# A graph layer by sorted running sums: each engine's order written out as lists, and scores taken by quarters of columns

## The chip, the cores and the metric

The kernel runs on one core of one Trainium2 chip. The metric is the time on the device in microseconds (us); lower is better. Before the change it is 2181.99 us, the median of three runs (2181.45 to 2182.83).

## What is computed

For each of B = 32 batches, `x` is a matrix of C = 512 rows (nodes) and N = 1024 columns. Two layers follow each other, each with a residual and a layer norm over the columns:

```python
# layer 0: attention whose score is a sum of one term per row and one per column
q = wq @ x[b];  k = wk @ x[b]                      # N values each
scores[m, n] = leaky_relu(q[n] + k[m])             # slope 0.01
agg = x[b] @ softmax(scores, axis=n).T
x1 = layernorm(x[b] + relu(adj @ agg + bm[:, None]))
# layer 1: adjacency again, its elements squared
out = layernorm(x1 + (adj * adj).T @ x1 + bias)
```

The softmax of such a sum needs no N x N matrix. For a given m, exp(leaky(q[n] + k[m])) is a product of a factor of n and a factor of m on either side of the sign change. So the kernel sorts the columns by q, builds running sums over the sorted columns from both ends, and looks up for each m the two sums at the place where the sign changes.

## The kernel before

Tiles have 128 partitions. CT = 4 is the number of row blocks of `x`, NT = 8 the number of column blocks, and `x` stays in SBUF for about four batches (`xp`, 4 buffers).

Each batch passes these stages. The short names in brackets are those of the lists that the change introduces; the text uses them with batch and index, so that `t.7.0` is turn 0 of batch 7.

1. **Scores.** `load` [ld] brings x in four DMAs. `scores_parts` [pa, copy pc] multiplies each row block by `wqk`, which holds wq and wk in two of 32 columns; the four row blocks use the four 32-column tiles of TensorE (L167) and are copied out by ScalarE (L173). `scores_cols` [co, copy cc] turns the result with eight 128 x 128 transposes (L180) and adds the four parts on VectorE (L183). `scores_row` [ro, copy rc] spreads q over all partitions by eight more transposes (L191) and copies it with its maximum (L194).
2. **Ranks and counts.** `ranks` [rk, end re] counts on VectorE for each column how many q's come ahead of it (L206). `counts` [ct, ends ce and we] does so on ScalarE for the place of the sign change (L218), then takes the factors of m (Exp, L229).
3. **Product and scatter.** `product` [z, copy zc] computes adj times x for one column block (L241, four matmuls of 512 columns, PSUM to `zt` by ScalarE, L245). `scatter` [sc] writes the rows of `zt` to DRAM at their ranks, by an indirect DMA that GpSimd issues (L250).
4. **Sums.** `sums_load` [sl] reads the sorted rows back in two DMAs; `sums_exp` [se], `sums_up` [u] and `sums_down` [d] form the running sums of eight columns in each partition on VectorE (L284, L293). `carry` [cu and cd, copies uc and dc] adds up over partitions by matmuls (L310, copied out by L311); `table_up` [tu, te] and `table_down` [td] add the carries (L316), and the table goes to DRAM in two large DMAs and a small one [tw, tl].
5. **Lookup.** `gather` [g] fetches 128 table rows by an indirect DMA (L339), eight in a batch. `mix_weights` [mw] (L352 to L356) and `mix` [ms on ScalarE L361, mx on VectorE L362] combine the two sums.
6. **Layer 0 end.** `layer0` turns the mixed rows back [t, eight transposes each, L389], adds relu and residual on VectorE [r, L390] and takes the mean (L369); `layer0_spread` [s0] sums squares on ScalarE (L374), `layer0_root` and `layer0_end` [rt, rce] give the inverse deviation, by which the squared adjacency is scaled [w, L409].
7. **Layer 1.** `layer1` [l, row block m, half h; L418] multiplies, `layer1_out` adds the bias [b, L428], `layer1_spread` sums squares [s1] and takes the root on GpSimd [r1, L380, L381, L440], `layer1_scale` normalizes [n, L444], `layer1_store` writes [st].

Each engine runs its instructions in the order in which the program issues them; there is no scheduler (`manual_schedule`). One loop over i sets this order: iteration i has the product of batch i, the scores of i + 1, the lookup of i - 1 and the layers' end of i - 2, with a few steps of i - 3. The same code serves the first and last iterations, by conditions on i. SP issues all plain loads and stores in that order, GpSimd all indirect DMAs. [...]`p2` has three buffers of two banks (scores, turns, layer 1), `p1` two buffers of one bank (product, carries).

Of the kernel before, what the change touches and what calls it, by code (L numbers as in the profile page):

```python
# [25 lines left out]
F32 = mybir.dt.float32  # L26
# [14 lines left out]
def adj_resnorm_kernel(  # L41
# [15 lines left out]
    NH = N // H  # L57
# [8 lines left out]
    s3 = ctx.enter_context(tc.tile_pool(name="s3", bufs=3))  # L66
    dr = ctx.enter_context(tc.tile_pool(name="dr", bufs=1, space=bass.MemoryType.DRAM))
    p2 = ctx.enter_context(tc.tile_pool(name="p2", bufs=3, space=bass.MemoryType.PSUM))
    p1 = ctx.enter_context(tc.tile_pool(name="p1", bufs=2, space=bass.MemoryType.PSUM))
# [10 lines left out]
    load(0)  # L80

# [55 lines left out]
    def weights():  # L137
        nc.vector.tensor_scalar(nbm, nbm, -1.0, None, ALU.mult)
        for r, a in enumerate(adj_in):
            t = p1.tile([P, CT, P], F32, tag="m", name=f"adj_tp_{r}")  # L140
            for c in range(CT):
                nc.tensor.transpose(t[:, c, :], a[:, c * P : (c + 1) * P], ident)
            nc.vector.tensor_copy(adj_t[:, :, r * P : (r + 1) * P], t)
        for r, a in enumerate(adj_in):
            nc.vector.tensor_tensor(adj_2[:, r, :], a[:, 0:C], a[:, 0:C], ALU.mult)
            nc.vector.tensor_tensor(
                adj_2[:, r, r * P : (r + 1) * P], adj_2[:, r, r * P : (r + 1) * P], ident, ALU.add
            )
# [7 lines left out]
    class Batch:  # L156
        pass
# [4 lines left out]
    def scores_parts(b):  # L162
        s, xt = st[b], xts[b]
        t4 = p2.tile([P, N], F32, tag="w", name=f"qk_ps_{b}")
        for h in range(NH):
            for c in range(CT):
# [80 lines left out]
    def scatter(b, j):  # L247
# [7 lines left out]
        )  # L255


    def sums_load(b):


        s = st[b]
# [319 lines left out]
```

## Time and profile before

| | |
|---|---|
| median of 3 runs | 2181.99 us |
| profiled execution, its own time | 2177.85 us |
| its span, first to last instruction | 2176.1 us |
| mean granted TensorE clock | 0.981 |
| TensorE (PE) busy | 2078.4 us, 96% |
| VectorE (DVE) busy | 1678.2 us, 77% |
| ScalarE (ACT) busy | 1277.4 us, 59% |
| GpSimd (POOL) busy | 901.3 us, 41% |
| DMA | 541.53 MB, mean 249 GB/s |

The profile comes from one execution. Its slices divide the span into 40 equal parts and give the busy share in tenths, 9 meaning 90% or more. A group line gives source line, engine, operation, output and inputs, the count, the busy time with the mean of one instruction, and the idle time ahead with what ended it. In order of time, a line gives start, length, engine, source line and operation, and in brackets the idle time ahead with its releaser. PE's instructions overlap, so that the difference of two starts is a better price than the length of one.

### The profile page before, as it was taken

The page shows a single profiled execution, that of the slowest core. Times are in us where ns is not written, and L with a number is a line of the kernel's source. Part 1 is how long each engine was busy: PE and PEld are TensorE (multiplying, and loading weights), DVE is VectorE, ACT ScalarE, POOL GpSimd, SP SyncE. Part 2 cuts the span into 40 slices and gives each one's busy share as a digit, 9 for nine tenths or more (in the row PEclk, how much of TensorE's full clock was granted, in tenths as well). Part 3 has the DMA queues.
Part 4 walks back from the last instruction along what each step waited for, and adds up shares of the span by engine and source line. Part 5 has one row for each costly group of instructions (what it writes and reads, how often), then busy time and mean ns, then how long its engine had stood idle before and what let it go on. Part 6 is the DMA issues. An engine that isn't in the chain of part 4 may idle for free. (4 is left out here: it accounts for less than half of the span.)

```text
span 2176.1 us, 21481 instructions
## 1 busy us (share of the span) xinstructions
PE 2078.4 (96%) x6416; PEld 1008.9 (46%) x6416; DVE 1678.2 (77%) x2965; ACT 1277.4 (59%) x2142; POOL 901.3 (41%) x1037
## 2 busy tenths in 40 slices
PE   5759999999999999999999999999999999999976
PEld 2324444444444444444444444444444444444433
DVE  4677877878778878878787977787887788787562
ACT  2346666556666556666655666655666665566443
POOL 1223445444344434444543434443444453444431
PEclk9879999999999999999999999999999999999988
DMA  3566787666787667678777668776667866766751
GB/s 121 197 227 234 268 300 265 253 254 230 256 292 290 250 256 255 236 274 301 258 255 263 237 245 296 284 260 252 252 237 272 300 257 252 256 241 255 258 197 68
DMA packets 139705, 541.53 MB, mean 249 GB/s; under 512 B 16034, under 2 KB 16034, under 8 KB 131396
## 3 DMA queue, kind: packets, MB, share of 16 engines
q1 hardware_dynamic: 79936, 336.42, 40.8%
q0 software_dynamic: 57344, 202.15, 27.4%
q10 hardware_dynamic: 2308, 1.58, 0.2%
q8 instruction: 51, 0.84, 0.1%
q14 instruction: 66, 0.54, 0.1%
HBM read 270.80 MB, written 269.29 MB: 248 GB/s over the span
## 5 line engine op out<-in xcount | busy, mean ns | idle before, releaser
L241 PE MATMUL z_ps<-adj_t,x 128*128 128x512 f32 x2048 | 916.1, 598 | 5.2 <-ACT zt L245 4.3
L418 PE MATMUL l_ps<-x,w 128*128 128x512 f32 x2048 | 894.1, 595 | 16.8 <-DVE w L409 16.8
L418 PEld LDWEIGHTS l_ps<-x,w 128*128 128x128 f32 x2048 | 390.7, 191 | 496.6 <-issue 492.0
L241 PEld LDWEIGHTS z_ps<-adj_t,x 128*128 128x128 f32 x2048 | 380.8, 191 | 474.7 <-issue 451.3
L250 POOL DMA_INDIRECT sorted_z<-zt,to x256 | 275.6, 1076 | 408.5 <-ACT zt L245 235.9
L380 POOL TENSOR_SCALAR sd<-var 128x1 f32<-128x1 f32 x128 | 93.1, 728 | 702.4 <-ACT junk L374 701.1
L206 DVE SCALAR_TENSOR_TENSOR junk_v<-qk,qkc,tie 128x1024 uint8<-128x1024 f32 x256 | 328.3, 1283 | 7.0
L339 POOL DMA_INDIRECT got<-table,of x256 | 268.1, 1047 | 132.8 <-issue 69.9
L390 DVE SCALAR_TENSOR_TENSOR x<-agg_ps,nbm,x 128x1024 f32<-128x1024 f32 x128 | 163.9, 1280 | 179.8 <-PE agg_ps L389 179.8
L218 ACT ACTIVATE junk_s<-qk,qkc 128x1024 bf16<-128x1024 f32 x256 | 294.2, 1149 | 13.8 <-DVE qk L194 9.6
L444 ACT ACTIVATE g<-g,nb,rs 128x1024 f32<-128x1024 f32 x128 | 158.9, 1241 | 179.4 <-POOL spare L473 91.8
L245 ACT COPY zt<-z_ps 128x512 f32<-128x512 f32 x256 | 148.6, 581 | 179.2 <-PE z_ps L241 178.9
L361 ACT ACTIVATE got<-got,w 128x512 f32<-128x512 f32 x256 | 163.4, 709 | 112.4 <-DVE w L356 112.4
L381 POOL TENSOR_TENSOR rs<-sd,power 128x1 f32<-128x1 f32 x128 | 217.4, 1698 | 10.7
L374 ACT ACTIVATE junk<-x,nmean 128x1024 bf16<-128x1024 f32 x128 | 147.3, 1151 | 96.6 <-DVE nmean L369 95.7
L362 DVE SCALAR_TENSOR_TENSOR got<-got,w 128x512 f32<-128x512 f32 x256 | 175.1, 746 | 35.4 <-ACT got L361 35.4
L374 ACT ACTIVATE junk<-g,nmean 128x1024 bf16<-128x1024 f32 x128 | 146.3, 1143 | 92.9 <-DVE nmean L369 92.1
L428 DVE SCALAR_TENSOR_TENSOR g<-l_ps,bias_b 128x1024 f32<-128x1024 f32 x128 | 156.3, 1221 | 31.2 <-PE l_ps L418 30.3
L293 DVE SCALAR_TENSOR_TENSOR tab<-tab,ac 128x513 f32<-128x513 f32 x224 | 168.6, 753 | 8.0
L389 PEld LDWEIGHTS agg_ps<-ident,got 128*128 128x128 f32 x1024 | 121.1, 143 | 70.3 <-issue 62.2
L284 DVE SCALAR_TENSOR_TENSOR tab<-tab,ac 128x514 f32<-128x514 f32 x192 | 144.9, 755 | 9.7 <-ACT ac L273 1.3
L316 DVE TENSOR_TENSOR tab<-tab,carry 128x2052 f32<-128x2052 f32 x64 | 143.8, 2288 | 0.0
(76 smaller groups left out, 1315.5 us busy)
## 6 DMA issues: line engine op xcount, KB each, us to landing
table<-tab SPq DMA_DIRECT2D x64, 2056.0 KB
tab<-sorted_z SPq DMA_DIRECT2D x64, 1028.0 KB
x<-in_x_dram SPq DMA_DIRECT2D x128, 512.0 KB
out_dram<-g SPq DMA_DIRECT2D x128, 512.0 KB
sorted_z<-zt,to POOLq DMA_INDIRECT x256, 5.4
got<-table,of POOLq DMA_INDIRECT x256, 5.8
adj<-in_adj_dram ACTq DMA_DIRECT2D x4, 256.0 KB
bias_b<-in_L_gnn_bias_dram ACTq DMA_DIRECT2D x1, 512.0 KB
```

What stands on the lines that cost most here:

```text
L206: nc.vector.scalar_tensor_tensor(junk, s.qb, s.q[:, j : j + 1], tie[:, at : at + N], ALU.subtract, ALU.is_gt, accum_out=s.rank[:, j : j + 1],)
L218: nc.scalar.activation(junk, s.qb, AF.Sign, bias=s.k[:, j : j + 1], accum_out=s.sign[:, j : j + 1])
L241: nc.tensor.matmul(t, xt[:, c, j * P : (j + 1) * P], adj_t[:, c, :], start=(c == 0), stop=(c == CT - 1),)
L250: nc.gpsimd.indirect_dma_start(out=sorted_z[b % 2][:, :], out_offset=bass.IndirectOffsetOnAxis(ap=s.to[:, j : j + 1], axis=0), in_=zt[:, j ...
L293: nc.vector.scalar_tensor_tensor(zs[:, j, 0:D], zs[:, j, 0:D], s.ac[:, 1, j : j + 1], zs[:, j + 1, 0:D], ALU.mult, ALU.add,)
L339: nc.gpsimd.indirect_dma_start(out=s.got[:, j, :], out_offset=None, in_=table[b % 2][:, :], in_offset=bass.IndirectOffsetOnAxis(ap=s.of[:, ...
L361: nc.scalar.activation(down, down, AF.Copy, scale=w[:, 1, j : j + 1])
L362: nc.vector.scalar_tensor_tensor(up, up, w[:, 0, j : j + 1], down, ALU.mult, ALU.add)
L374: nc.scalar.activation(junk, t, AF.Square, bias=v[1][:, i : i + 1], accum_out=v[2][:, i : i + 1])
L381: nc.gpsimd.tensor_tensor(v[4][:, at], v[3][:, at], power[:, at], ALU.pow)
L390: nc.vector.scalar_tensor_tensor(t[:, o, :], ps, nbm[:, o : o + 1], t[:, o, :], ALU.max, ALU.add, accum_out=s.v0[0][:, o : o + 1],)
L418: nc.tensor.matmul(s.ps[m][:, at], s.w2[:, n, m * P : (m + 1) * P], t[:, n, at], start=(n == 0), stop=(n == CT - 1),)
```

## The change

The loop with its conditions is gone. Every step is a small function with a short name, and three lists of words give the order in which the steps are issued: `head` for the first batches, `loop`, which is repeated 17 times, and `tail` for the last. A word is a step's name, a batch relative to a base, and the step's indices; the base is 0 for the head, 10 to 26 for the loop and 32 for the tail, so that `t.-3.0` in the loop with base 10 is `t.7.0`, and `l.-2.0.0` in the tail is `l.30.0.0`. Steps that were one function are now two where they run on two engines (a product and its copy, a mix's scaling and its sum). The order of each engine, SP and GpSimd included, follows from the lists alone.

The scores change too. `parts` gives each of the four column tiles of TensorE a quarter of the columns instead of a row block, and sums over the row blocks in PSUM; two transposes are then enough, and VectorE copies instead of adding. The means are no longer computed apart: the Square takes the plain sum as its bias and -N as its scale, and the root divides by N cubed. `p1` now has four buffers and `p2` two. At the start, the three weight vectors come as rows and are turned on TensorE, the adjacency comes in one DMA on SP ahead of x, its squares are formed on GpSimd, half of the copies of the turned adjacency go to ScalarE, and the bias is loaded from inside the head list.

The diff, cut to its core:

```diff
-    p2 = ctx.enter_context(tc.tile_pool(name="p2", bufs=3, space=bass.MemoryType.PSUM))
-    p1 = ctx.enter_context(tc.tile_pool(name="p1", bufs=2, space=bass.MemoryType.PSUM))
+    p2 = ctx.enter_context(tc.tile_pool(name="p2", bufs=2, space=bass.MemoryType.PSUM))
+    p1 = ctx.enter_context(tc.tile_pool(name="p1", bufs=4, space=bass.MemoryType.PSUM))
...
+    adj_in = one.tile([P, NT, 2 * ZR], F32, tag="got", name="adj_in")[:, 0:CT, 0:C]
+    nc.sync.dma_start(out=adj_in, in_=adj.rearrange("(r p) c -> p r c", p=P))
+    load(0)
...
-    def scores_parts(b):
-        s, xt = st[b], xts[b]
-        t4 = p2.tile([P, N], F32, tag="w", name=f"qk_ps_{b}")
-        for h in range(NH):
-            for c in range(CT):
-                nc.tensor.matmul(
-                    t4[32 * c : 32 * c + 32, h * H : (h + 1) * H], wqk[:, c, :],
-                    xt[:, c, h * H : (h + 1) * H], start=True, stop=True,
                 )
...
+    def parts(b):
+
+        s = st[b]
+        s.ps = p1.tile([P, C], F32, tag="m", name=f"qk_ps_{b}")[:, 0:Q]
+        for c in range(CT):
+            for g in range(CT):
+                nc.tensor.matmul(
+                    s.ps[32 * g : 32 * g + 32, :], wqk[:, c, :],
+                    xts[b][:, c, g * Q : (g + 1) * Q], start=(c == 0), stop=(c == CT - 1),
                 )
...
+    def cols(b):
+        s = st[b]
+        s.ps = p1.tile([P, C], F32, tag="m", name=f"qk_tp_{b}")[:, 0:Q]
+        for k in range(Q // P):
+            at = slice(k * P, (k + 1) * P)
+            nc.tensor.transpose(s.ps[:, at], s.part[:, at], ident)
...
-    def mean(i, v):
-        nc.vector.tensor_scalar(v[1][:, i : i + 1], v[0][:, i : i + 1], -1.0 / N, None, ALU.mult)
...
         nc.scalar.activation(
-            junk, t, AF.Square, bias=v[1][:, i : i + 1], accum_out=v[2][:, i : i + 1]
+            junk, t, AF.Square, bias=v[0][:, i : i + 1], scale=-float(N),
+            accum_out=v[1][:, i : i + 1],
         )
...
-        nc.gpsimd.tensor_scalar(v[3][:, at], v[2][:, at], 1.0 / N, EPS, ALU.mult, ALU.add)
-        nc.gpsimd.tensor_tensor(v[4][:, at], v[3][:, at], power[:, at], ALU.pow)
...
+        nc.gpsimd.tensor_scalar(v[1][:, at], v[1][:, at], 1.0 / N**3, EPS, ALU.mult, ALU.add)
+        nc.gpsimd.tensor_tensor(v[1][:, at], v[1][:, at], power[:, at], ALU.pow)
...
-    for i in range(B + 3):
-        new, cur, old, past = i + 1 < B, i < B, 0 <= i - 1 < B, 0 <= i - 2 < B
...
+    def emit(words, base):
+        for word in words.split():
+            name, b, *at = word.split(".")
+            ops[name](base + int(b), *map(int, at))
+            if name in pool_ops:
+                pool_last[0] = "scatter" if name == "sc" else None
+
+    head = """
+    ld.1 ld.2 pa.0 z.0.1 pc.0 co.0 zc.0.1 pa.1 cc.0 z.0.6 ro.0 z.0.0 rc.0 rk.0.0 ct.0.3 ct.0.4
+    rk.0.3 z.0.2 ct.0.7 rk.0.2 pc.1 oq.0 ct.0.2 rk.0.5 z.0.3 zc.0.0 rk.0.1 zc.0.2 zc.0.6 rk.0.6
+    rk.0.7 z.0.4 zc.0.3 ct.0.6 rk.0.4 re.0 sc.0.0 co.1 zc.0.4 z.0.5 cc.1 ct.0.5 sc.0.6 ct.0.1
+    sc.0.2 sc.0.4 ro.1 zc.0.5 ct.0.0 sc.0.1 z.0.7 ce.0 sc.0.5 rc.1 we.0 sc.0.3 rk.1.3 z.1.3
+    zc.0.7 ct.1.4 sc.0.7 rk.1.4 rk.1.1 z.1.0 rk.1.2 sl.0.0 rk.1.5 sl.0.1 ld.3 oq.1 rk.1.7 z.1.6
+    rk.1.6 rk.1.0 se.0.0 z.1.1 ct.1.7 u.0.0 u.0.1 zc.1.3 u.0.2 se.0.1 zc.1.6 u.0.3 zc.1.0 pa.2
...
+    z.3.7 ms.0.5 d.1.3 zc.3.0 mx.0.3 ms.0.7 d.1.2 zc.3.3 zc.3.6 mx.0.5 mx.0.7 cu.1 d.1.1 z.3.2
+    uc.1 mx.0.6 zc.3.7 mx.0.4 tu.1.1 t.0.0 d.1.0 t.0.1 r.0.0 cd.1 r.0.1 t.0.3 dc.1 oq.3 s0.0.1
+    t.0.2 td.1.1 sc.3.3 z.3.1 s0.0.0 r.0.2 zc.3.2 tw.1.1 r.0.3 s0.0.2 z.3.5 tu.1.0 s0.0.3 rt.0
+    td.1.0 z.3.4 we.1 rce.0 tw.1.0 w.0.0 w.0.3 w.0.1 w.0.2 te.1 l.0.3.0 tl.1 l.0.1.0 sl.2.0
+    g.1.0 sl.2.1 g.1.1 l.0.3.1 g.1.3 g.1.2 g.1.6 l.0.1.1 b.0.3 g.1.5 s1.0.3 g.1.4 ct.3.5 l.0.0.0
+    b.0.1 g.1.7 se.2.0 zc.3.4 u.2.0 sc.3.0 zc.3.5 u.2.1 sc.3.7 se.2.1 u.2.2 ct.3.3 l.0.2.0
...
+    u.2.6 ms.1.3 mx.1.0 s1.0.1 u.2.7 l.0.2.1 ct.3.2 r1.0.1 mx.1.3 mw.1.1 b.0.0 ms.1.4 ms.1.7
+    r1.0.3 mx.1.2 ms.1.6 cu.2 ld.4 mx.1.4 ms.1.5 mx.1.7 s1.0.0 mx.1.5 mx.1.6 r1.0.0 b.0.2 t.1.1
+    d.2.7 s1.0.2 t.1.0 r.1.1 uc.2 r1.0.2 r.1.0 t.1.3 n.0.1 d.2.6 n.0.3 t.1.2 d.2.5 sc.3.1 s0.1.0
+    z.4.0 d.2.4 sc.3.2 n.0.0 d.2.3 s0.1.1 d.2.2 st.0.0 st.0.3 r.1.2 pa.4 n.0.2 d.2.1 st.0.2
+    z.4.2 ce.3 d.2.0 we.3 s0.1.2 r.1.3 pc.4 zc.4.0 te.2 tu.2.1 cd.2 tl.2 zc.4.2 st.0.1 co.4 dc.2
...
+    loop = """
+    g.-3.3 rk.-1.1 ct.-1.4 g.-3.4 rk.-1.0 g.-3.6 z.-1.3 rk.-1.5 g.-3.7 b.-4.0 g.-3.5 oq.-1
+    rk.-1.6 l.-4.2.0 se.-2.0 rk.-1.4 u.-2.0 u.-2.1 l.-4.3.0 mw.-3.0 rk.-1.3 ms.-3.1 zc.-1.3
+    se.-2.1 re.-1 u.-2.2 ms.-3.2 l.-4.2.1 ms.-3.0 mx.-3.1 zc.-1.2 mx.-3.0 ct.-1.1 mx.-3.2 u.-2.3
+    l.-4.3.1 b.-4.2 mw.-3.1 u.-2.4 ms.-3.4 ms.-3.7 u.-2.5 l.-4.1.0 ms.-3.3 mx.-3.4 ms.-3.6
+    u.-2.6 ms.-3.5 b.-4.3 ct.-1.6 mx.-3.6 s1.-4.0 l.-4.1.1 mx.-3.5 s1.-4.3 mx.-3.3 r1.-4.0
+    mx.-3.7 s1.-4.2 u.-2.7 t.-3.0 d.-2.7 ld.0 ct.-1.7 r1.-4.2 d.-2.6 cu.-2 ct.-1.5 b.-4.1 z.-1.0
+    d.-2.5 s1.-4.1 sc.-1.3 d.-2.4 r.-3.0 r1.-4.3 t.-3.2 zc.-1.0 d.-2.3 uc.-2 z.-1.1 n.-4.2
+    d.-2.2 sc.-1.0 d.-2.1 st.-4.2 r1.-4.1 d.-2.0 r.-3.2 t.-3.1 zc.-1.1 n.-4.0 cd.-2 tu.-2.1
+    sc.-1.1 st.-4.0 t.-3.3 dc.-2 n.-4.3 sc.-1.2 pa.0 r.-3.1 ct.-1.0 st.-4.3 td.-2.1 z.-1.6
+    ct.-1.3 s0.-3.0 te.-2 tw.-2.1 r.-3.3 z.-1.7 tu.-2.0 s0.-3.3 zc.-1.6 td.-2.0 s0.-3.1 sc.-1.6
+    z.-1.5 pc.0 s0.-3.2 tw.-2.0 tl.-2 rt.-3 co.0 zc.-1.7 z.-1.4 rce.-3 cc.0 zc.-1.5 w.-3.0
+    n.-4.1 w.-3.2 w.-3.1 ce.-1 st.-4.1 w.-3.3 l.-3.0.0 zc.-1.4 we.-2 sc.-1.4 sc.-1.5 ro.0
+    sc.-1.7 z.0.2 rc.0 g.-2.0 g.-2.2 ct.0.2 rk.0.7 g.-2.1 sl.-1.0 rk.0.2 l.-3.0.1 sl.-1.1
+    """
+    tail = """
...
+    zc.-1.3 mx.-3.5 l.-4.2.1 dc.-2 sc.-1.3 mx.-3.7 td.-2.1 z.-1.5 b.-4.2 tw.-2.1 td.-2.0 t.-3.0
+    zc.-1.5 tu.-2.0 s1.-4.2 t.-3.1 ct.-1.6 r.-3.0 z.-1.4 r1.-4.2 tw.-2.0 st.-4.0 r.-3.1 s0.-3.0
+    sc.-1.5 t.-3.2 zc.-1.4 s0.-3.1 sc.-1.4 t.-3.3 r.-3.2 n.-4.2 r.-3.3 l.-4.1.0 s0.-3.2 st.-4.2
+    te.-2 s0.-3.3 ce.-1 tl.-2 we.-1 sl.-1.0 rt.-3 sl.-1.1 l.-4.1.1 rce.-3 g.-2.0 g.-2.2 w.-3.0
+    g.-2.1 w.-3.2 se.-1.0 w.-3.3 w.-3.1 b.-4.1 g.-2.3 l.-3.3.0 g.-2.5 u.-1.0 s1.-4.1 u.-1.1
+    g.-2.4 u.-1.2 se.-1.1 l.-3.3.1 g.-2.6 u.-1.3 u.-1.4 g.-2.7 u.-1.5 u.-1.6 l.-3.2.0 u.-1.7
+    mw.-2.0 d.-1.7 ms.-2.2 b.-3.3 ms.-2.1 l.-3.2.1 ms.-2.3 d.-1.6 ms.-2.0 mx.-2.1 d.-1.5 mx.-2.0
+    l.-3.1.0 mx.-2.2 mw.-2.1 mx.-2.3 ms.-2.5 b.-3.2 ms.-2.6 ms.-2.7 mx.-2.6 l.-3.1.1 s1.-3.2
+    mx.-2.7 d.-1.4 ms.-2.4 s1.-3.3 mx.-2.5 d.-1.3 r1.-3.3 mx.-2.4 d.-1.2 t.-2.0 b.-3.1 r1.-3.2
+    d.-1.1 n.-3.3 t.-2.2 r.-2.0 cu.-1 d.-1.0 t.-2.1 s0.-2.0 r1.-4.1 r.-2.2 cd.-1 uc.-1 r.-2.1
+    t.-2.3 s0.-2.2 tu.-1.1 l.-3.0.0 s0.-2.1 dc.-1 n.-4.1 r.-2.3 s1.-3.1 st.-4.1 td.-1.1 l.-3.0.1
+    s0.-2.3 r1.-3.1 td.-1.0 tw.-1.1 rt.-2 n.-3.1 rce.-2 tu.-1.0 w.-2.0 tw.-1.0 w.-2.2 w.-2.3
+    w.-2.1 b.-3.0 l.-2.0.0 te.-1 s1.-3.0 tl.-1 n.-3.2 r1.-3.0 l.-2.2.0 st.-3.2 st.-3.3 g.-1.0
+    l.-2.0.1 g.-1.1 g.-1.2 g.-1.3 l.-2.2.1 b.-2.0 g.-1.4 g.-1.5 l.-2.3.0 b.-2.2 g.-1.6 mw.-1.0
+    g.-1.7 ms.-1.3 ms.-1.2 l.-2.1.0 ms.-1.0 n.-3.0 mx.-1.0 mx.-1.2 ms.-1.1 st.-3.0 s1.-2.0
+    st.-3.1 mx.-1.1 l.-2.3.1 mx.-1.3 s1.-2.2 r1.-2.0 mw.-1.1 ms.-1.7 ms.-1.6 mx.-1.7 ms.-1.4
+    l.-2.1.1 mx.-1.6 r1.-2.2 ms.-1.5 b.-2.3 mx.-1.5 mx.-1.4 n.-2.2 b.-2.1 t.-1.0 r.-1.0 t.-1.1
+    r.-1.1 t.-1.2 s0.-1.0 r.-1.2 t.-1.3 s0.-1.1 r.-1.3 s0.-1.2 s0.-1.3 rt.-1 s1.-2.3 rce.-1
+    w.-1.0 w.-1.2 s1.-2.1 w.-1.3 w.-1.1 n.-2.0 l.-1.1.0 r1.-2.1 st.-2.0 n.-2.1 l.-1.0.0 st.-2.1
+    st.-2.2 l.-1.1.1 l.-1.0.1 b.-1.1 s1.-1.1 r1.-1.1 l.-1.2.0 b.-1.0 s1.-1.0 r1.-2.3 l.-1.3.0
+    r1.-1.0 n.-2.3 l.-1.2.1 st.-2.3 n.-1.0 n.-1.1 l.-1.3.1 b.-1.2 st.-1.1 st.-1.0 s1.-1.2
+    r1.-1.2 b.-1.3 s1.-1.3 n.-1.2 r1.-1.3 st.-1.2 n.-1.3 st.-1.3
+    """
     weights()
...
+    emit(head, 0)
+    for b in range(10, B - 5):
+        emit(loop, b)
+    emit(tail, B)
```

## The prediction

> **What bounds the kernel now.** I read the page's slices first, then the time in stretches of 64 us, then TensorE in order of time.
>
> ```profile
> PE   5759999999999999999999999999999999999976
> DVE  4677877878778878878787977787887788787562
> ```
>
> TensorE is full from slice 5 to slice 38; VectorE nowhere is.
>
> ```profile
> 64.00:128.00 64.00, 38.83 (x111) 17.53 (x109) 38.32 (x61) 26.10 (x51) 21.67 (x24) 0.82 0.61 228
> 128.00:192.00 64.00, 49.68 (x162) 24.94 (x163) 47.17 (x80) 30.58 (x55) 16.90 (x19) 0.86 0.67 242
> 1024.00:1088.00 64.00, 63.97 (x201) 31.16 (x200) 51.83 (x93) 39.60 (x68) 28.90 (x32) 1.00 0.71 257
> 2048.00:2112.00 64.00, 48.33 (x130) 24.23 (x130) 43.00 (x75) 26.34 (x43) 20.61 (x21) 0.84 0.59 221
> 2112.00:2176.00 64.00, 45.63 (x123) 21.37 (x121) 20.33 (x45) 26.72 (x37) 7.60 (x24) 0.87 0.16 66
> ```
>
> The columns after the length are PE, PEld, DVE, ACT, POOL, then granted clock, DMA share and GB/s. In mid-run PE has 63.97 of 64 us. At both ends it has 39 to 50, at a lower clock too. So two things can shorten this kernel: less PE work in each batch, and fewer holes at the ends.
>
> ```profile
> 729.40 3.70 PE L241 MATMUL z_ps<-adj_t,x 128*128 128x512 f32 x8
> 732.94 1.04 PE L389 MATMUL agg_ps<-ident,got 128*128 128x128 f32 x8
> 733.90 1.92 PE L167 MATMUL qk_ps<-x,wqk 128*32 128x512 f32 x16
> 735.76 3.70 PE L241 MATMUL z_ps<-adj_t,x 128*128 128x512 f32 x8
> 739.30 1.04 PE L389 MATMUL agg_ps<-ident,got 128*128 128x128 f32 x8
> 740.17 1.04 PE L180 MATMUL qk_tp<-ident,qk 128*128 128x128 f32 x8
> 741.04 3.60 PE L241 MATMUL z_ps<-adj_t,x 128*128 128x512 f32 x8
> ```
>
> From start to start this prices PE: z 3.43 us for a j, parts (L167) 1.86, eight transposes 0.87. A half of `layer1` is 3.43 and a carry 0.87 by the same view. The first z after a layer 1 begins at 724.03 in this batch and at 788.30 in the next: the period is **64.27 us**. The sum is 8 x 3.43 + 8 x 3.43 + 4 x 0.87 + 2 x 0.87 + 1.86 + 0.87 + 0.87 = 63.7, so 0.55 us a batch are small waits.
>
> ```profile
> 142.29 2.05 PE L310 MATMUL carry_ps<-end,before 128*128 128x257 f32 x4 [23.55 <-DVE end L284]
> ...
> 2093.57 29.98 PE L418 MATMUL l_ps<-x,w 128*128 128x512 f32 x64 [10.37 <-DVE w L409]
> 2123.39 3.97 PE L389 MATMUL agg_ps<-ident,got 128*128 128x128 f32 x32
> 2133.76 30.36 PE L418 MATMUL l_ps<-x,w 128*128 128x512 f32 x64 [6.40 <-DVE w L409]
> ```
>
> The holes: PE waits for chains on VectorE that have no other PE work over them. The steady order begins at 209.20 (batch 3's first z); the PE work done by then is worth 134 us (three batches of z 82, one layer 1 27.5, four scores 14.5, turns, carries, weights 10), so the **start costs 75 us**. After 2010.53 there remain 122 us of PE work (z 27.5, three layer 1 82.5, turns and carries 12), and PE ends at 2164: 31 us lost, and 12 more to the span's end. The **end costs 43 us**. Check: 32 x 63.7 + 2 + 75 + 43 + 28 x 0.55 = 2174, against a span of 2176.1.
>
> **What the Trainium skill says.** "TensorE: Matmul & The Clock Gate", Part 3 (packing small matmuls), says that matmuls in different column tiles run at once. The trace agrees: 16 passes of 0.592 us each take 1.86 us together. The same page, Part 1, says an idle window halves the PE clock; the clock of 0.82 to 0.87 beside the holes agrees. "Perfetto Trace Analysis", Optimizing Tensor Performance, says that independent groups should rotate through PSUM banks; the waits list has the next z's load waiting for a carry's copy (L311) 30 times, 13.0 us in all, with two `p1` buffers.
>
> **The change part by part.**
>
> *Scores by quarters.* Parts go from 8 matmuls of 512 columns to 16 of 256, c outside and the four column tiles inside. A 257-column pass takes 0.380 us against 0.592 (carry rows), and four carry passes 0.87. Packed four wide, 8 groups x 0.218 = 1.74; nearest row 1.86; unpacked 32 x 0.218 = 7.0. I take 1.86, no gain. The sum over c is now in PSUM, so `cols` is 2 transposes, not 8: 6 x 0.109 = **0.65 us a batch off PE**, 21 us in all. The copy out is 256 columns (0.375 by the L311 row) for two of 0.578, and DVE's reduce of 0.217 becomes a copy of like size; both lie beside PE work.
>
> *No separate means.* 256 instructions of L369 go, 39.4 us of DVE, 1.2 a batch. The Square takes the sum as its bias and -N as a constant scale; root and `nb` keep three POOL operations. Nothing on PE waits for a mean in mid-run, since DVE is busy 51.8 of 64. Worth: 0.15 on each chain at the ends. I count nothing, between -1 and +1 us.
>
> *PSUM.* `p1` has 4 buffers, `p2` 2. `p1` frees the waits for carry copies (0.4 of the 0.55). With two, `p2` needs `biased` or `residual` prompt: in the loop list `l.6.1.0` waits for `b.6.2` (1.30 us) while `l.6.3.1` runs 3.43 us. Cost 0 while that cover holds.
>
> *Loop order* (names with base 10, position 0 at its start, PE units added up). The list has z and layer 1 mixed. Three covers decide. (1) `t.7.3` ends at 36; then `r.7.3` behind `td.8.1`, four Squares among two counts, a table load with Sqrt (1.6) and four `w` (1.7) end near 50.2; `l.7.0.0` is due at 52. (2) `ld.10` follows `l.6.1.1` at 24 and `pa.10` is at 36: 12 us, where now 9.7 (724.22 to 733.90) suffice. (3) Eight gathers stand together on POOL behind `sc.9.7`, from about -6.5, beside the two sums loads. The last batch now shows such a burst alone: begun near 2095.5, `w` released at 2110.78, 15.2 us for 4.2 MB. With 2.1 MB of sums, 21 us at 300 GB/s, the rate of the busiest slices: they land at 14.5. `mw.7.1` and its mixes need about 9, `t.7.0` is due at 24. All three are covered, the first and third by one or two us. On SP, `ld.10` stands ahead of the stores and of both table writes, which are issued from 39 and 45: its wait ends at 24. On POOL the four `r1` (2.7 each) stand ahead of scatters whose last goes at 56. I take 0.7 us of waits a period, between 0.2 and 2.
>
> *Start.* The copies of the turned adjacency are shared by DVE and ACT (0.69 each), its squares move to POOL, whose first scatter comes near 43, and the bias is loaded on SP behind the first table write (0.5 MB; first read at 160): nothing for these, up to 2 us if POOL is slow. x0 landed at 15.9; now the 1 MB of adjacency is ahead of it on SP's queue instead of beside it on ACT's: PE begins near 17. `pa.1` waits 3 us for x1. Then z of batches 0 to 3 cover the first chain: PE has 115 us of listed work ahead of `t.0.0`, t = 134. On DVE, ranks and sums end near 67, the table is written near 100, gathers are in at 115, mixes end near 132. `l.0.3.0`, at 151, needs `w` by 148. One wait has no cover: `ld.4` is behind the whole of layer 1 of batch 0 and `z.4.0` comes 4.3 us later, where a load takes 9.7: 5 us. With 2 for clock, **27 instead of 75**.
>
> *End.* Now three layer 1 are left after the last z, with holes. In the list, at `z.31.4`, 103 us of PE work are left, in which the last batch's table and gathers lie. Two holes stay: `l.30.0.0` comes 6.9 us (two halves of `l.29.0`) after `t.30.3`, whose chain is about 12: 5 us; `l.31` behind `t.31`: 6.4 as now. With 2 for slow clock, 2 for `t.31` behind gathers, 12 after the last matmul: **27 instead of 43**.
>
> *Sum.* 32 x 63.05 = 2017.6, weights 2, start 27, end 27, 27 periods x 0.7 = 19: span 2092.6. The profiled run lies 1.75 over its span (2177.85 against 2176.1): 2094. The median of before is 4.1 over its profiled run, so about 2098; I forecast **2096**.
>
> **The rivals.**
>
> *The periods gain nothing.* Cover (1) or (3) fails by up to 2.5 us: a period of 64.3 to 66.3. For: one or two us is less than POOL's L381 varies (1.1 to 2.5 us in one batch). Against: DVE has 12 us free in each. 27 x 0.6 to 2.5 more: 2112 to 2165. The ends still gain.
>
> *The ends fill half.* The lists count on chains that start on time, and an engine in order behind one late load delays all. 75 + 43 then go to about 86 instead of 54: 2128.
>
> *Slower: the gather burst.* Gathers, sums loads and table writes meet, and `t.7.0` waits for mixes in every period. It decides from 3.1 us of added wait a period (84 us / 27). If the 6.3 MB move at 250 GB/s (25 us) and the table lands 3 us later, the burst ends at 21.7, the mixes at 30.7, and `t.7.0`, due at 24, stalls 6.7 us in each period, 6 more than I keep: 2096 + 27 x 6 = 2258. Against: the DMA share is 0.71 now at 257 GB/s.
>
> *The quarters don't pack.* Parts serial, 7.0: 32 x 5.1 = +163, 2259. Against: the column tiles are the same as now.
>
> **How the numbers follow.** Forecast 0.60 (2070 to 2114), no gain in periods 0.20, half-filled ends 0.11, burst 0.07, no packing 0.02. The range is 2070 to 2148: it keeps the forecast, the second and most of the first rival. 0.2% is 4.4 us, about what a measurement of this kernel can tell from no change. Only the last two cases and a little of the first are slower: faster 0.89, same 0.02, slower 0.09.
>
> **What would show it.** Right: L167's successor with 1024 passes of about 0.38 and about 1.9 us a batch; `qk_tp` with 64 transposes; a period near 63.7; PE at 9 from the second slice; a wait of about 5 us for x near 180; holes of some 5 and 6 us before the last two layer 1. Wrong: a period over 65, with PE waiting for `w` or `got`; parts of several us; a DMA share that rises while PE idles.

## The result, and the profile after

The changed kernel takes **2082.72 us**, the median of 4 runs (2081.17 to 2087.41), against 2181.72 us (2181.39 to 2182.83) for the kernel before, measured beside it: a ratio of 0.9549, with a 95% interval of 0.9532 to 0.9566. It is faster by 99 us. The profiled execution took 2081.17 us, its span is 2079.4 us and its mean granted clock 0.994.

The slices of the page of the changed kernel, to be held against those of before:

```profile
PE   8999999999999999999999999999999999999986
DVE  4879879777788777788777887777887778777762
PEclk9999999999999999999999999999999999999998
```

TensorE is now full from the second slice on; before it was so from the fourth. VectorE has the same share of a shorter span. Only the last two slices still dip. The time in stretches of the changed kernel (the columns after the length are PE, PEld, DVE, ACT, POOL, granted clock, DMA share, GB/s):

```profile
64.00:128.00 64.00, 64.00 (x211) 31.48 (x210) 56.84 (x95) 37.05 (x70) 31.71 (x38) 1.00 0.63 239
128.00:192.00 64.00, 62.64 (x217) 31.05 (x216) 49.62 (x77) 38.65 (x68) 23.07 (x33) 1.00 0.74 288
1024.00:1088.00 64.00, 64.00 (x213) 31.39 (x212) 49.85 (x85) 38.28 (x67) 28.00 (x33) 1.00 0.69 267
1952.00:2016.00 64.00, 57.68 (x156) 26.72 (x155) 43.77 (x73) 29.06 (x49) 26.99 (x31) 0.97 0.65 248
2016.00:2080.00 64.00, 46.72 (x124) 21.50 (x122) 20.88 (x41) 30.49 (x42) 8.28 (x24) 0.87 0.27 107
```

Where PE had 38.83 and 49.68 of 64 us in the second and third stretch before, it has 64.00 and 62.64, and at full clock. At the end the last stretch but one gains (57.68 against 48.33), and the last is much as it was (46.72 against 45.63). TensorE of the changed kernel in order of time, in mid-run:

```profile
1039.17 1.04 PE L432 MATMUL agg_ps<-ident,got 128*128 128x128 f32 x8
...
1051.37 1.93 PE L171 MATMUL qk_ps<-x,wqk 128*32 128x256 f32 x32
1053.23 10.57 PE L260 MATMUL z_ps<-adj_t,x 128*128 128x512 f32 x24
1063.64 0.38 PE L186 MATMUL qk_tp<-ident,part 128*128 128x128 f32 x2
1063.85 3.60 PE L260 MATMUL z_ps<-adj_t,x 128*128 128x512 f32 x8
...
1102.50 1.04 PE L432 MATMUL agg_ps<-ident,got 128*128 128x128 f32 x8
```

From `t.x.0` to `t.x.0` is 1102.50 - 1039.17 = **63.33 us**. Before, the period was 788.30 - 724.03 = 64.27 us, from the first product after a layer 1 to the next:

```profile
724.03 3.60 PE L241 MATMUL z_ps<-adj_t,x 128*128 128x512 f32 x8
...
788.30 3.60 PE L241 MATMUL z_ps<-adj_t,x 128*128 128x512 f32 x8
```

The score parts take 1053.23 - 1051.37 = 1.86 us, as before, and the transposes of the columns 0.21 instead of 0.87. The same view, where PE still waits (the bracket gives the idle time ahead of the line and what ended it):

```profile
171.08 1.09 PE L432 MATMUL agg_ps<-ident,got 128*128 128x128 f32 x8 [0.63 <-DVE g L480]
...
1908.57 5.40 PE L260 MATMUL z_ps<-adj_t,x 128*128 128x512 f32 x8 [3.37 <-ACT zt L266]
...
1998.26 29.43 PE L469 MATMUL l_ps<-x,w 128*128 128x512 f32 x64 [2.83 <-DVE w L460]
...
2036.75 30.68 PE L469 MATMUL l_ps<-x,w 128*128 128x512 f32 x64 [3.94 <-DVE w L460]
```

The two holes at the start in which carries waited 39.2 us together, 23.55 of it in the one shown before, are gone; after the 7.01 us that TensorE waits for its first load, the largest is now 3.94 us. The two `layer1` at the end take 29.43 and 30.68 us for work that takes 27.5 in mid-run: there the clock is below full.

### The profile page after: what moved, and what is told of

Same layout as the page of the kernel before. It is cut to its first block, busy times and chain, and to the rows that moved or that the text cites. A ratio compares the mean times of both kernels' runs of the same rounds, so it can differ in the third digit from the quotient of the medians.

```text
span 2079.4 us, 21612 instructions
## 1 busy us (share of the span) xinstructions
PE 2042.6 (98%) x6737; PEld 1000.6 (48%) x6737; DVE 1609.8 (77%) x2700; ACT 1234.2 (59%) x2112; POOL 881.8 (42%) x1083
## 5 line engine op out<-in xcount | busy, mean ns | idle before, releaser
L274 POOL DMA_INDIRECT sorted_z<-zt,to x256 | 356.4, 1392 | 465.7 <-ACT zt L266 304.6
L234 ACT ACTIVATE junk_s<-qb,qkc 128x1024 bf16<-128x1024 f32 x256 | 293.5, 1146 | 104.0 <-DVE qb L211 99.9
L382 POOL DMA_INDIRECT got<-table,of x256 | 275.9, 1078 | 160.8 <-issue 75.0
L221 DVE SCALAR_TENSOR_TENSOR junk_v<-qb,qkc,tie 128x1024 uint8<-128x1024 f32 x256 | 328.3, 1282 | 5.8
L425 POOL TENSOR_SCALAR var<-var 128x1 f32<-128x1 f32 x128 | 37.6, 294 | 535.4 <-ACT junk L418 530.8
L409 DVE SCALAR_TENSOR_TENSOR got<-got,w 128x512 f32<-128x512 f32 x256 | 181.7, 747 | 24.1 <-ACT got L404 18.8
L418 ACT ACTIVATE junk<-g,tot 128x1024 bf16<-128x1024 f32 x128 | 146.8, 1147 | 48.4 <-DVE g L480 43.0
L497 ACT ACTIVATE g<-g,nb,var 128x1024 f32<-128x1024 f32 x128 | 158.4, 1244 | 10.6 <-POOL nb L491 10.6
L418 ACT ACTIVATE junk<-x,tot 128x1024 bf16<-128x1024 f32 x128 | 147.0, 1149 | 16.2 <-DVE x L440 11.3
L432 PE MATMUL agg_ps<-ident,got 128*128 128x128 f32 x1024 | 133.0, 274 | 5.5 <-DVE g L480 2.3
```

The lines of the kernel that those rows point to most:

```text
L221: nc.vector.scalar_tensor_tensor(junk, s.qb, s.q[:, j : j + 1], tie[:, at : at + N], ALU.subtract, ALU.is_gt, accum_out=s.rank[:, j : j + 1],)
L234: nc.scalar.activation(junk, s.qb, AF.Sign, bias=s.k[:, j : j + 1], accum_out=s.sign[:, j : j + 1])
L274: nc.gpsimd.indirect_dma_start(out=sorted_z[b % 2][:, :], out_offset=bass.IndirectOffsetOnAxis(ap=s.to[:, j : j + 1], axis=0), in_=zt[:, j ...
L382: nc.gpsimd.indirect_dma_start(out=s.got[:, j, :], out_offset=None, in_=table[b % 2][:, :], in_offset=bass.IndirectOffsetOnAxis(ap=s.of[:, ...
L409: nc.vector.scalar_tensor_tensor(up, up, s.w[:, 0, j : j + 1], down, ALU.mult, ALU.add)
L418: nc.scalar.activation(junk, t, AF.Square, bias=v[0][:, i : i + 1], scale=-float(N), accum_out=v[1][:, i : i + 1],)
```

## The experiments

Each run is given as its ratio to the kernel before with the 95% interval; 0.001 is 2.2 us. The changed kernel stands at 0.9549 in these terms. "The period" is the distance of the first products after a layer 1 in mid-run; for kernels with the loop list, a pass is the distance from `t.x.0` to the next.

### The quarters alone

```diff
-        for h in range(NH):
-            for c in range(CT):
-                    t4[32 * c : 32 * c + 32, h * H : (h + 1) * H], wqk[:, c, :],
+        for c in range(CT):
+            for g in range(CT):
+                    t4[32 * g : 32 * g + 32, :], wqk[:, c, :],
...
-        for j in range(NT):
-            nc.tensor.transpose(t[:, j * P : (j + 1) * P], s.qk4[:, j * P : (j + 1) * P], ident)
+        for k in range(Q // P):
+            nc.tensor.transpose(t[:, k * P : (k + 1) * P], s.qk4[:, k * P : (k + 1) * P], ident)
```

> The kernel before with the scores by quarters alone (sixteen matmuls of 256 columns summed over the row blocks in PSUM, two transposes, one copy), in the old order and with the old PSUM split. My theory: six transposes of 0.109 us leave TensorE in each batch and the parts stay at 1.86 us, 0.65 us x 32 = 21 us, ratio 0.9904 (2161). Rival, the period is set by more than TensorE's sum, so that the gap is filled by a wait: ratio 0.997 to 1.000. Second rival, the copies that go (one of 0.578 on ScalarE, shorter ones) open more waits than they were counted for: under 0.988.

Measured 0.9977 (0.9964 to 0.999): 5 us instead of 21, the rival's size. The profiled execution (2168.2 us) is among the fastest of ten (2167.2 to 2179.0), so its trace shows less of the loss than the median has. Of 20 periods in mid-run 11 last 63.62 us, exactly the forecast 0.65 less than 64.27, and the others 64.1 to 65.1. The waits of TensorE in this kernel name what takes the place (total, times, longest):

```profile
PE qk_tp L181 <- ACT qk L173: 7.5, 13, 1.1
```

The two transposes wait for ScalarE's copy of the parts. ScalarE in order of time, in a period without such a wait:

```profile
1118.08 1.24 ACT L447 ACTIVATE g<-g,nb,rs 128x1024 f32<-128x1024 f32 x1 [3.33 <-POOL spare L476]
1119.22 0.35 ACT L173 COPY qk<-qk_ps 128x256 f32<-128x256 f32 x1
```

The copy stands behind a normalization of the layer before last, which has waited 3.33 us for GpSimd's root. It ends at 1119.57; the transposes come at 1119.84. The margin is 0.3 us even in this good period.

### The copy ahead of the normalization

```diff
+            if j == 1 and new:
+                scores_parts(i + 1)
             if j == 1 and last:
                 layer1_scale(i - 3, CT - 1)
...
-                if j == 1:
-                    scores_parts(i + 1)
```

> The kernel before with the scores by quarters, as in the run with quarters alone, and one step moved on ScalarE: the copy of the score parts stands ahead of the normalization of the fourth row block (which waits for GpSimd's root) instead of behind it. TensorE's order is the same. My theory: in the run with quarters alone TensorE waited in 8 of 20 periods up to 1.3 us for that copy, and this was what ate the gain; with the copy ahead each period is 63.62 and the gain is the predicted 21 us: ratio 0.989 to 0.991. Rival, another late step takes the place of that wait (the next product's copy, or the columns' copy on VectorE): ratio 0.994 to 0.998 as with quarters alone.

Measured 0.9987 (0.9979 to 0.9994). My theory fell: the wait for the copy is all but gone, and nothing more is gained. The waits of TensorE in this kernel:

```profile
PE carry_ps L313 <- DVE end L287: 44.4, 9, 24.2
...
PE carry_ps L313 <- ACT zt L248: 9.9, 13, 0.9
```

The carries wait instead: for the end of the running sums on VectorE (9 times against 2 in the kernel before, where these two are the holes at the start, as they are some 40 of the 44.4 us here) and for a product's copy (13 times). The mean period is 64.3 again. So a second limit stands just behind TensorE in the old order, and it does not consist of that one copy. It shows as lateness: the first exponents of a batch's sums start on average 13.3 us after the end of its last product on TensorE in the kernel before, 14.9 with the quarters, and 16.5 here (batches 6 to 25). As TensorE got shorter, everything beside it came later relative to it, until something else waited.

### The quarters without the means

```diff
-        mean(o, s.v0)
...
-            junk, t, AF.Square, bias=v[1][:, i : i + 1], accum_out=v[2][:, i : i + 1]
+            junk, t, AF.Square, bias=v[0][:, i : i + 1], scale=-float(N),
+            accum_out=v[2][:, i : i + 1],
```

> The kernel before with the scores by quarters and without the separate means, in the old order, with the old PSUM split and the old start. My theory: in the old order a second limit stood just behind TensorE, the chain of mixes, sums, running sums and tables on VectorE, which the quarters alone did not shorten; the eight means of 0.15 us are 1.2 us of it in each batch, so without them the period is TensorE's 63.62 and the quarters pay in full: 20 to 23 us, ratio 0.989 to 0.991. Rival, the means hide beside TensorE's work as the prediction said, and the gain of the changed functions in the old order came from the score parts' own tiles and the start loads: ratio 0.996 to 0.999, as with quarters alone.

Measured 0.9885 (0.987 to 0.99), 25 us: the theory's mechanism, and slightly more than it had. Every period from the fourth on is 63.62 us, as from 1161.49 to 1225.11, the first exponents are back at 13.8 us, and of the wait for the copy one of 0.5 us is left:

```profile
PE qk_tp L181 <- ACT qk L173: 0.5, 1, 0.5
...
1161.49 3.60 PE L244 MATMUL z_ps<-adj_t,x 128*128 128x512 f32 x8
...
1225.11 3.60 PE L244 MATMUL z_ps<-adj_t,x 128*128 128x512 f32 x8
```

The means, which the prediction counted at nothing, decide in the old order whether the quarters pay 5 us or 25. That the second limit yields when the eight means of a batch (1.2 us of VectorE) go is shown. Whether it is their time on VectorE or the wait of ScalarE's Squares for them was not separated, which links of the chain of mixes, sums and tables make up the limit was not followed, and no run takes the means out without the quarters: these stay open.

### The PSUM split alone

```diff
-    p2 = ctx.enter_context(tc.tile_pool(name="p2", bufs=3, space=bass.MemoryType.PSUM))
-    p1 = ctx.enter_context(tc.tile_pool(name="p1", bufs=2, space=bass.MemoryType.PSUM))
+    p2 = ctx.enter_context(tc.tile_pool(name="p2", bufs=2, space=bass.MemoryType.PSUM))
+    p1 = ctx.enter_context(tc.tile_pool(name="p1", bufs=4, space=bass.MemoryType.PSUM))
```

> The kernel before with the other PSUM split alone: p1 with four buffers of one bank, p2 with two of two banks. My theory: in the old order a turn, a score part or a half of layer 1 often asks for a third p2 buffer, while carry copies cost only 0.4 us a period, so the split does not pay by itself: a period 0 to 3 us longer, ratio 1.00 to 1.04. Rival, the split gains what the prediction gave it, 0.4 us x 28 = 11 us: ratio 0.995.

Both splits fill eight banks, 3 x 2 + 2 and 2 x 2 + 4. Measured 1.0092 (1.0069 to 1.0115): 20 us slower. The waits of TensorE in this kernel:

```profile
PE l_ps L418 <- DVE g L428: 24.8, 17, 3.5
```

A block of `layer1` asks for a p2 buffer while VectorE has not yet added the bias to the last but one. The old order loses by two. The split also does what it is for: the wait of the next product's weights for a carry's copy, 30 times and 13.0 us in the kernel before, is gone, and the shortest periods are 63.97 us.

### The old order with all the rest changed

The lists are replaced by one list with the order of the kernel before, once with the new split, once with the old one.

```diff
-    emit(head, 0)
-    for b in range(10, B - 5):
-        emit(loop, b)
-    emit(tail, B)
+    emit(words, 0)
```

> The changed kernel with only the order undone: the same small steps, quarters, no means and PSUM split, but issued in the order of the kernel before, for all 32 batches. My theory: the order is worth most of the gain, start about 58 us (75 against 14 to 17) and end about 6, plus some of the period: 2145 to 2165, ratio to before 0.983 to 0.992. Rival, the quarters, means and PSUM split carry half of it: 2120 to 2135, ratio 0.972 to 0.978.

> The same with the old PSUM split too (p1 two buffers, p2 three): quarters, no means and the new start loads in the old order. My theory: like quarters alone, since means are worth 0 to 1 us and the start loads about 5 us: 2152 to 2162, ratio 0.987 to 0.991. Rival, the means on the chains at the ends and in mid-run are worth more: under 2145. The difference to the run with the new split says what the split is worth in the old order.

Measured 0.9956 (0.9942 to 0.997) and 0.9874 (0.986 to 0.9888). The second is the run of quarters without means (0.9885) with the new start loads and more buffers for a few small tiles added; the difference lies within the intervals. The first is 18 us slower than the second, and slower than I expected, by the wait that the split alone showed:

```profile
PE l_ps L469 <- DVE g L480: 36.4, 26, 3.8
```

In undisturbed periods the first is the faster one: its shortest are 63.32 us against 63.62. That is what four p1 buffers gain in the same order.

So order and split together are worth 0.9874 - 0.9549 = 0.0325, some **71 us**, against the old order with the split that suits it. With the new split in both, the order alone is worth 0.9956 - 0.9549 = 0.0407, some 89 us: it is also what makes the new split bearable.

### The old order at one end only

> The changed kernel with the loop and the tail as they are, and only the steps of the head issued in the order of the kernel before. My theory: the start costs 75 us in that order against 14, of which the new start loads keep about 5; two p2 buffers cost some 4 more: 55 to 62 us longer, 2137 to 2145, ratio to before 0.979 to 0.983. Rival, the prediction's figure for the start (75 against 27): about 48 us, 2130. Second rival, most of the start is the new loads and not the order: under 2110.

> The changed kernel with the head and the seventeen passes of the loop as they are, and only the last batches issued in the order of the kernel before. My theory: the end costs 43 us in the old order against about 37 in the new one, and two p2 buffers cost the old order some 0.9 us a period for some four periods: 6 to 12 us longer, 2089 to 2095, ratio to before 0.957 to 0.960. Rival, the prediction's figures (43 against 27): 16 us or more longer, 2099 and above. Second rival, the lists for the end gain nothing: 2081 to 2085.

For the first, the head's steps are issued in the old order, and loop and tail are kept; for the second, head and loop are kept and the rest is issued in the old order.

```diff
-    emit(head, 0)
-    for b in range(10, B - 5):
-        emit(loop, b)
-    emit(tail, B)
+    emit(words, 0)
```

The old head gives 0.9805 (0.9791 to 0.982), a span of 2135.6 us: 56 us longer, as expected. TensorE in order of time there:

```profile
63.03 2.05 PE L330 MATMUL carry_ps_True<-end,before 128*128 128x257 f32 x4 [15.73 <-DVE end L312]
...
121.53 2.05 PE L330 MATMUL carry_ps_True<-end,before 128*128 128x257 f32 x4 [23.42 <-DVE end L312]
```

These are the two holes of the kernel before, 39 of the 56 us: with no products of batches 1 to 3 to put over the first sums, TensorE stands still.

The old tail gives 0.9687 (0.9673 to 0.9702), a span of 2109.5 us: 30 us longer, where I expected 6 to 12. TensorE in order of time there:

```profile
1602.72 13.47 PE L469 MATMUL l_ps<-x,w 128*128 128x512 f32 x24 [8.51 <-DVE g L480]
...
1677.25 5.15 PE L469 MATMUL l_ps<-x,w 128*128 128x512 f32 x8 [3.26 <-DVE g L480]
...
2067.21 30.45 PE L469 MATMUL l_ps<-x,w 128*128 128x512 f32 x64 [5.08 <-DVE w L460]
```

The first two are the seam: the loop leaves the batches at other stages than the old order expects. The waits at the seam (8.51, 0.57, 0.33, 3.26) are 12.7 us, and beside the first the granted clock falls to 0.53 (1598 to 1609). At the first turn of batch 26 TensorE stands 20.5 us further behind its listed work than in the changed kernel (1753.73 and 1739.23 us, the work issued by then taken off); 2 of these are from a longer pass of the loop. So some 18 us of the 30 are the seam, and some 10 are what the old order with two p2 buffers loses over the last batches against the list, which is the size that I expected. Order and split are not separated within these 10.

The parts agree with the whole: 56 us for the head, some 10 for the last batches, and 17 passes at 63.33 us against a mean period of 64.6 in the old order with the new split, 22, are 88 of the 89 us.

### The eight transposes put back

```diff
-            nc.tensor.transpose(s.ps[:, at], s.part[:, at], ident)
+            for _ in range(4):
+                nc.tensor.transpose(s.ps[:, at], s.part[:, at], ident)
```

> The changed kernel with each of the two column transposes done four times over, so that TensorE has the eight transposes of before in each batch again. My theory: in the new order TensorE sets the period in all batches, so six transposes of 0.109 us cost in full: 0.65 x 32 = 21 us, 2102 to 2105, ratio to before about 0.965. Rival, a chain beside TensorE sets the period here too, as it did in the old order, and the added work fills its waits: 2084 to 2092.

Measured 0.9728 (0.9711 to 0.9744), 2118.5 us: the passes of the loop take 63.98 to 63.99 us against 63.33, the forecast 0.65 more, so in the loop TensorE sets the period. But the whole is 35 us between the profiled spans (39 by the ratios), not 21. A pass, and the waits of TensorE in this kernel, which hold part of the rest:

```profile
1314.31 1.04 PE L433 MATMUL agg_ps<-ident,got 128*128 128x128 f32 x8
...
1378.30 1.04 PE L433 MATMUL agg_ps<-ident,got 128*128 128x128 f32 x8
...
PE l_ps L470 <- DVE g L481: 9.0, 5, 3.0
```

Two passes of the loop lasted 65.5 and 67.5 us (more below), and in head and tail the longer TensorE work opened new waits of 1 to 5 us: there the lists fit the durations that they were written for closely.

### The means put back

```diff
+    def mean(i, v):
+        nc.vector.tensor_scalar(v[0][:, i : i + 1], v[0][:, i : i + 1], -1.0 / N, None, ALU.mult)
...
+        mean(o, s.v0)
```

> The changed kernel with the means computed on VectorE again (256 instructions of about 0.15 us). My theory: the lists leave VectorE's chains room in each period, so nothing is lost in the loop and up to 3 us at the two ends: 2083 to 2087, ratio to before 0.955 to 0.957. Rival, the chains are as tight as in the old order (the w of layer 1 come about 1 us ahead of their use): 0.3 to 1.2 us a period more, 2092 to 2118.

Measured 0.9577 (0.9561 to 0.9593), 2088.45 us. The passes of the loop take 63.33 us, as without means, but for two of 65.5 and 66.2. So the lists leave VectorE room in all passes of the loop but two; what the means cost in the profiled execution is some 3 us at the ends and 5 in those two passes, in which TensorE waits for a bias and for the end of the running sums. The intervals of this run and of the changed kernel overlap a little.

### Three p1 buffers

```diff
-    p1 = ctx.enter_context(tc.tile_pool(name="p1", bufs=4, space=bass.MemoryType.PSUM))
+    p1 = ctx.enter_context(tc.tile_pool(name="p1", bufs=3, space=bass.MemoryType.PSUM))
```

> The changed kernel with three p1 buffers instead of four (p2 keeps two). My theory: in the loop a score part, its columns or a carry hold a buffer while products rotate through the others, so that with three a product waits for the copy of the one but two before it, when ScalarE is at a Square or a normalization: 0.3 to 1.5 us a period, 2090 to 2120. Rival, the fourth buffer only bridges what two buffers could not, and three do: 2081 to 2086.

Measured 0.9624 (0.9609 to 0.9639), 2097.7 us. The loop loses 0.07 us a pass (63.40), far less than expected; nearly all of the 16 us is lost in head and tail, where several products stand in a row:

```profile
PE z_ps L260 <- ACT zt L266: 12.8, 7, 8.1
```

With two p1 buffers and three p2 (I had expected 0.5 to 4 us a period more) the lists can't run at all, so there is no time. The loop list shows why. `cu.-2`, a carry, takes both p1 buffers. On TensorE `z.-1.0` comes next that needs one, and waits for the carry's copy `uc.-2`. On ScalarE `uc.-2` stands behind `zc.-1.0`, the copy of that very product, so each waits for the other. The lists need at least three p1 buffers; the cost of the old split in this order is not a time but a deadlock.

### The largest hole at the end

In the changed kernel ScalarE waits for the sums of batch 30, with three copies of the last batch's products queued behind:

```profile
1907.56 0.30 ACT L298 ACTIVATE ac<-tab,top 128x4 f32<-128x4 f32 x1 [7.70 <-DMA tab<-sorted_z]
```

```diff
-    se.-2.0 z.-1.0 g.-3.6 w.-4.3 w.-4.1 zc.-1.1 u.-2.0 zc.-1.2 g.-3.5 rk.-1.0 g.-3.7 u.-2.1
-    z.-1.6 w.-4.2 se.-2.1 u.-2.2 zc.-1.7 ct.-1.4 u.-2.3 u.-2.4 l.-4.0.0 zc.-1.6 rk.-1.7 u.-2.5
+    zc.-1.1 z.-1.0 g.-3.6 w.-4.3 w.-4.1 w.-4.2 zc.-1.2 zc.-1.7 se.-2.0 u.-2.0 g.-3.5 rk.-1.0 g.-3.7 u.-2.1
+    z.-1.6 ct.-1.4 se.-2.1 u.-2.2 u.-2.3 u.-2.4 l.-4.0.0 zc.-1.6 rk.-1.7 u.-2.5
```

> The changed kernel with six words of the list for the last batches moved: on ScalarE the copies of three products of the last batch stand ahead of the exponents of batch 30's sums instead of behind them, and on VectorE the fourth w of batch 28 ahead of the running sums. In the changed kernel the exponents wait 7.7 us for the sums to land, and a product behind them waits 3.4 us for a p1 buffer. My theory: that wait goes, and since the last batch's products, scatters and sums follow from it, 2 to 3.4 us of it reach the end of the span: span 2076 to 2077.5, median 2079 to 2081. Rival, the later holes are set by the landing of the sums and gathers, not by the product: the wait turns up again behind the next products, span 2079 to 2080.

Measured 0.9549 (0.9527 to 0.9571), 2082.44 us: no difference to the changed kernel. The hole of 3.37 us is gone and another stands in its place:

```profile
1929.21 5.21 PE L469 MATMUL l_ps<-x,w 128*128 128x512 f32 x8 [4.25 <-DVE g L480]
```

The landing of the sums holds VectorE as well as ScalarE, and the biases of `layer1` queue behind the running sums. It is the rival's case in kind; the spans of the five runs, 2076.4 to 2083.3 us, spread too widely to tell a gain of 2 us by themselves.

This execution also shows what goes with a longer pass of the loop. Stretches of 10 us, the first two from a pass of 64.9 us, the last from the next, of 63.3:

```profile
700.00:710.00 10.00, 10.00 (x25) 4.39 (x24) 7.20 (x17) 1.69 (x4) 1.84 (x2) 1.00 0.97 383
710.00:720.00 10.00, 8.90 (x22) 3.77 (x21) 7.18 (x14) 6.70 (x13) 0.00 (x0) 1.00 0.02 8
...
763.00:773.00 10.00, 10.00 (x25) 4.47 (x24) 9.04 (x20) 3.27 (x9) 3.17 (x4) 1.00 1.03 404
```

The DMA engines are busy nearly all the time, at 383 GB/s, and PE waits (1.09 us, for a bias on VectorE to free a p2 buffer) just as they fall idle. The two sums loads were issued at 692.99 and 757.68. The first exponents start at 703.66 and 763.47, 10.7 and 5.8 us later, and in the long pass those of the second half only at 710.93. The short pass has as full a burst of gathers and sums; what sets the long one apart is that its sums came in 5 us later. It looks like the burst, a rival of the prediction, in a small form, but what delays the sums in one pass and not in the next is not shown. None of the passes of the profiled execution of the changed kernel is long, other variants have one or two that are longer by 0.9 to 3.5 us.

## Why the prediction was right, and where its terms were off

**The total.** The forecast was 2096 us, from a span of 2092.6; the span is 2079.4. Held against its own sum, 32 x 63.05 = 2017.6 and:

| term | forecast | measured |
|---|---|---|
| start and weights | 27 + 2 | about 18 |
| waits in 27 periods | 19 | 27 x (63.33 - 63.05) = 7.6 |
| end | 27 | about 36 |

The deviations are about -11, -11.4 and +9; they sum to the -13.2 that separate the spans. Start and end are the time at which TensorE stands less its listed work: 18 us at `t.5`, and 2079.4 - 2017.6 - 7.6 - 18 = 36 for the end. The total owes a little to luck: an end that was sized too small took back 9 of the 22 us by which start and periods were sized too large.

**Scores by quarters: right in size, with a condition that was not seen.** The parts kept their 1.86 us for 16 matmuls of 256 columns (32 passes in the trace) and the columns gave 0.65 us. "TensorE: Matmul & The Clock Gate", Part 3, of the Trainium skill says that matmuls packed into different tiles of the array run at once; the trace shows this for the new order of c and tile too. But 21 us are to be had only if nothing else has that length: in the old order the gain was 5 us. The prediction read 12 us of idle VectorE time a period as room, where a second limit was as long as TensorE's work.

**No separate means: "I count nothing" failed for the old order.** There they are worth 0.9977 - 0.9885 = 0.0092, 20 us, on top of the quarters. In the new order the step holds in most passes of the loop (63.33 with or without); putting them back cost 2088.45 - 2082.72 = 6 us in all, more than the 1 us that was allowed for, with intervals that just overlap.

**PSUM: right in the wait and the cover, a little high in size.** In one and the same old order, undisturbed periods take 63.62 us with two p1 buffers and 63.32 with four: 0.30 of the 0.4 us that the prediction gave it. What it did not see is that the lists need more than two. And "cost 0 while that cover holds" for the two p2 buffers is borne out by both sides: no wait in the loop of the profiled execution, 18 to 20 us lost in the order that lacks the cover (0.9956 against 0.9874, and 1.0092).

**Loop order: the three covers held,** more fully than the 0.7 us a period that was set aside. The first `layer1` to wait for a `w` is the one at 1958, and `l.x.0.0` starts 1.1 us after its `w` in mid-run (1003.96 after 1002.82; forecast 1.8). The margin of the gathers is as thin as the prediction put it, "by one or two us": in other variants single passes lose 1 to 3.5 us.

**Start: the mechanism right, three terms too large.** The forecast let PE begin near 17 behind the 1 MB of adjacency; the first parts started at 10.79. It had 3 us of wait for x1 and 5 for x4, "where a load takes 9.7". Both were zero: SP issued `ld.4` at 168.79, `z.4.0` started at 174.82, 6 us later, and its last matmuls, which read the fourth row block, at 177.40, without a wait. The step that failed is taking 9.7 us, the distance between issue and use in the kernel before, for the duration of a load; it was only an upper bound. `t.0.0` came at 125.93, not 134. That the order and not the new loads makes the start is shown by the old head, which has the new loads and loses 56 us. (Before, TensorE is full from the fourth slice; the prediction's "slice 5" is one too late, which nothing rests on.)

**End: the term that was too small.** The holes were forecast at 5, 6.4 and 2. After 1900 the waits of PE sum to 14.7, in ten pieces: the two that were named are 2.83 and 3.94, and a third of 3.37, a product behind the landing of the sums, was not foreseen. The 12 us after the last matmul are there (2067.4 to 2079.4). What failed is "2 for slow clock". The changed kernel's last batches in stretches, columns as above:

```profile
1900.00:1908.00 8.00, 5.20 (x13) 1.98 (x11) 2.55 (x6) 0.45 (x3) 4.12 (x4) 1.00 1.02 383
1908.00:1914.00 6.00, 5.43 (x9) 2.39 (x10) 4.06 (x7) 1.00 (x3) 0.00 (x0) 0.72 0.87 347
1914.00:1998.00 84.00, 77.42 (x232) 37.99 (x230) 71.15 (x113) 53.89 (x94) 36.22 (x42) 1.00 0.51 201
1998.00:2002.00 4.00, 3.74 (x5) 1.60 (x6) 3.23 (x7) 2.67 (x4) 0.36 (x2) 0.57 0.94 395
2002.00:2035.00 33.00, 30.04 (x92) 14.52 (x90) 16.56 (x32) 15.01 (x22) 10.77 (x17) 1.00 0.60 224
2035.00:2043.00 8.00, 6.25 (x8) 2.66 (x9) 1.85 (x5) 5.59 (x9) 1.00 (x3) 0.57 0.33 132
```

The clock falls three times, beside the three longest holes (1908.57, 1998.26 and 2036.75); by my estimate from these lines it takes 6 x 0.28 + 4 x 0.43 + 8 x 0.43 = 6.8 us, and 36 - 14.7 - 12 - 6.8 leaves 2.5 that no line names. The same page of the skill, "TensorE: Matmul & The Clock Gate", Part 1, says that the clock falls after idle windows. Here the holes of up to 1.44 us had no such stretch, but these runs give no length that decides: with the copies moved, the clock is 0.66 from 1986 to 1991, behind holes of 1.16 and 1.15 us, and full after one of 2.74. The old tail agrees that the list for the end does gain, by some 10 us with the seam taken off.

**The rivals.** No-gain periods, half-filled ends and unpacked quarters did not come about in the changed kernel; with the quarters alone in the old order, most of their gain was indeed lost. Something like the burst came, in single passes of other variants, at 1 to 3.5 us rather than the 6.7 in each.

## What to carry to other kernels

Here a cut in the busiest engine's work paid only down to a second limit close behind it, and the idle time of VectorE did not show that limit: read how late the other engines' steps come relative to the bound one, before and after. Buffers, order and work are priced together; the same PSUM split cost 20 us in one order, and the other can't run without its third p1 buffer. An order written out as a list fits the durations that it was written for: 0.65 us more a batch cost 35 to 39 us instead of 21, and mending a single hole moved it.

## What was not expected of the hardware

The load `ld.4`, 2.1 MB in four DMAs, was issued from 168.79 us on, and was read without a wait from 174.82 (first row block) to 177.40 (fourth). From 171 to 176 the DMA engines moved 401 GB/s, while the mean over the span is 260:

```profile
171.00:176.00 5.00, 4.29 (x27) 3.22 (x28) 4.93 (x10) 4.88 (x7) 2.98 (x6) 1.00 1.00 401
```

The same instruction of GpSimd, the power for one root of 128 x 1 values, took 2.48 us at 1994.00, while VectorE added carries to the table, and 0.55 us at 2070.46, with VectorE idle:

```profile
1994.00 2.48 POOL L426 TENSOR_TENSOR var<-var,power 128x1 f32<-128x1 f32 x1
...
2070.46 0.55 POOL L426 TENSOR_TENSOR var<-var,power 128x1 f32<-128x1 f32 x1
```

Sorted by what VectorE ran most of the time beside them, the 128 roots of the kernel before fall into three groups: 60 beside the additions to the table (L316) took 2.48 to 2.50 us, 60 beside the running sums (L284, L293) 0.89 to 1.09, and 8 with VectorE idle, at a bias or at a residual 0.55 to 0.57. The mean is 1.698 us there, 1.64 to 1.65 in the old order with all the rest changed, and 0.691 in the changed kernel, whose lists put most roots beside residuals and biases. So the order shortened them. That VectorE's instruction is the cause is what the sorting suggests; no run changes that instruction alone.
